# Max-pooling graph layer on one Trainium2 core: own-feature products of 34 node tiles made early, kept in DRAM and added by an identity product

## The chip, the cores and the metric

The program runs on one core of one Trainium2 chip. The metric is device time in microseconds (us) of one execution, from the hardware. Engines are named as in the profile: PE does matrix products (PEld loads their stationary operand), DVE and ACT do elementwise work, POOL issues the indirect gathers, SP and ACT issue direct DMAs (SPq and ACTq are their queues). Sixteen DMA engines move the data. On the printed clock column, PEclk 1.00 is the full TensorE clock.

## The reference

There are N = 6250 nodes with 256 features and E = 100000 edges, sorted by destination. The input is normalised, passed through a ReLU, and sent through four graph layers, then added to x:

```python
h = jnp.maximum(_layernorm(x, axis=-1), 0.0)
def _sage_mean(h, src, dst, n, deg, W_self, W_neigh, b):
    msum = jax.ops.segment_sum(h[src], dst, num_segments=n)
    return h @ W_self + (msum / jnp.clip(deg, 1.0)[:, None]) @ W_neigh + b
def _sage_pool(h, src, dst, n, deg, W_pool, b_pool, W_self, W_neigh, b):
    hp = jax.nn.relu(h @ W_pool + b_pool)
    hmax = jax.ops.segment_max(hp[src], dst, num_segments=n)
    hmax = jnp.where(deg[:, None] > 0, hmax, 0.0)
    return h @ W_self + hmax @ W_neigh + b
...
h = _sage_mean(features, edge_src, edge_dst, n, deg, W1_self, W1_neigh, b1)
h = _sage_pool(h, edge_src, edge_dst, n, deg, W2_pool, b2_pool, W2_self, W2_neigh, b2)
h = _sage_gcn(h, edge_src, edge_dst, n, deg, W3_neigh, b3)
h = _sage_mean(h, edge_src, edge_dst, n, deg, W4_self, W4_neigh, b4)
return h @ W_fc + b_fc
```

The case is about the second layer, `_sage_pool`: for each node the largest of its neighbours' rows `hp[src]`, times one matrix, plus the node's own features times another.

## The kernel before

Nodes lie in 49 tiles of 128 (tile d holds nodes 128d to 128d+127), edges in 782 groups of 128. Layer 1 leaves two tables in DRAM: `tab_p`, the rows `hp` of 512 floats, and `tab_t`, one 128x512 float block a tile that holds, transposed, the tile's normalised features and its neighbour mean (two 128-column pieces of each).

**The edge pass of layer 2** is the loop `for b in reversed(range(NB))` (L1679 on), over six blocks of edges, the last block first. Its counter `at` counts the 782 groups. For each, POOL gathers 128 rows of `tab_p` (256 KB) into a buffer `X` (L1688), DVE takes running maxima along the sorted edges (`step`, L1669: about one and a half instructions a group), and SP stores one of two rows back to DRAM (`rows<-X`, L1673). Six `X` buffers of two groups each rotate; a buffer is free again when its store has landed.

**Work issued beside the pass, at program points given by `at`:**
- up to `MADE_AT` = 64: products of weight matrices (`products2`), which give `usA`, `usB` (own features) and `unf` (maxima);
- `at` 17 to `EARLY_AT` = 310: `build_narrow` makes 14 blocks of an edge-count matrix for layer 3. For each, ACT makes one-hot rows (`ht` L375, `hs` L382), DVE others (`hm` L377), PE multiplies (`pb`, L393), ACT copies out (`A`, L398) and checks (`many`, L408). ACT stores the block (`tab_a`);
- from `at` = 112: `done2(d)` for tiles 48 down to 0, as their edge blocks are finished. `totals(d)` has POOL gather the maxima (`tot`, L1521) and ACT load the tile's `tab_t` block into `th` (L1527, a tag `th2` with four buffers). Then PE turns the maxima (L1545), ACT copies (L1548), PE adds up one PSUM bank `pm_prf`: the own-feature product from `th` with `usA` (L1552) and `usB` (L1555), and the maxima with `unf` (L1558). After that PE and ACT split the result into parts (L1567 to L1598) and ACT stores it (`tab_r`, L1599);
- after `at` = 320: `early_products`, layer-3 products of tiles 0 to 39 in batches of four. SP loads pieces of `tab_a` (`ae`, L1637), ACT widens them (`aw`, L1624), PE multiplies (`pd`, L574), DVE adds up (`acc`, L1306). Their buffers lie where `build_narrow` had its own, so they wait for its end.

The last tiles to be served go through `last_done2`, which places the own-feature product between the steps of the last carry (L1465). A scheduler turns program order into one in-order stream for each engine; within it an engine waits at the head of its stream.

A float product of 128x128 by 128x512 is one call in the code and shows in the trace as two MATMUL instructions; the own-feature product of a tile is four calls, eight instructions.

## Time and profile before

| what | value |
|---|---|
| median of 3 runs | 2745.0 us (2740.99 to 2750.39) |
| the profiled execution's own time | 2742.18 us |
| its span, first to last instruction | 2740.4 us |
| edge pass of layer 2 | first gather at 731.4 us, last at 1923.2 us |
| busy share of the span | PE 84%, DVE 76%, POOL 68%, ACT 47% |
| granted TensorE clock | 0.922 mean |

The profile is of one execution. Busy times of a window are read against its length; the idle time of an engine matters only where another waits for it. A row of the windows view gives, for each engine, busy time and number of instructions in that stretch, then the granted clock, the mean busy share of the 16 DMA engines and the rate that they moved. A row of the groups view gives line, engine, operation, out<-in, number | busy us, mean ns | idle time just before, with what ended it.

### The profile page before, as it was taken

To read this page: it belongs to the slowest core of one execution; us is meant where nothing else is said; L and a number is where in the kernel's file an instruction comes from. 1 tells how busy PE (TensorE), PEld (TensorE's weight loads), DVE (VectorE), ACT (ScalarE), POOL (GpSimd) and SP (SyncE) were. 2 spreads that over 40 slices of the span, in tenths; PEclk is the share of its full clock that TensorE was granted. 3 is DMA by queue.
4 is the path that set the end of the run, shared out by engine and by line. 5 is a ranking of instruction groups with operands and counts; after the bars stand their busy time and mean duration, and the time that the engine had idled before them with its cause. 6 is when DMAs were issued, how large, how long until landed. Compare 5 with 4: busy or idle time off the path is not lost.

```text
span 2740.4 us, 37738 instructions
## 1 busy us (share of the span) xinstructions
PE 2314.7 (84%) x10402; PEld 1439.0 (53%) x10402; DVE 2088.1 (76%) x5540; ACT 1299.7 (47%) x2859; POOL 1857.0 (68%) x2169
## 2 busy tenths in 40 slices
PE   4689999999786466566889999899799999789988
PEld 2356666767453232223555666655345444467776
DVE  8889777776589898898678998888376777446666
ACT  5568777764288888686423333232111111134443
POOL 5477777777566676677656676676477777657765
PEclk8799999999898588787999999999899999899999
DMA  8467777777799899899999999898899999999987
GB/s 279 152 179 209 209 208 213 217 232 221 222 356 333 299 346 336 283 336 361 328 290 301 339 349 322 275 341 292 300 376 387 381 380 351 347 323 316 319 286 226
DMA packets 365625, 809.90 MB, mean 296 GB/s; under 512 B 56238, under 2 KB 154646, under 8 KB 365372
## 3 DMA queue, kind: packets, MB, share of 16 engines
q0 software_dynamic: 143248, 501.86, 56.3%
q1 hardware_dynamic: 145928, 215.57, 21.6%
q10 hardware_dynamic: 76228, 89.96, 9.8%
q8 instruction: 85, 1.39, 0.2%
q14 instruction: 136, 1.11, 0.1%
HBM read 602.51 MB, written 205.46 MB: 295 GB/s over the span
## 4 chain that ended last, share of the span: by engine, by line
PE 48%; DMA 24%; DVE 13%; ACT 5%; issue 4%; POOL 2%; ACTq 0%; DVEq 0%; SPq 0%; POOLq 0%
PE pd L574 17%; PE pg L513 11%; DMA X<-rows,srcIf 7%; DMA xr<-in_x 4%; DVE run L1669 4%; DMA ring<-tab_h,srcT 4%; PE pm_hp L1175 3%; DMA rows<-X 3%; PE pm_prf L1558 3%; PE pm_hp L1169 2%; PE pd L566 2%; PE pb L349 2%; DVE acc L544 2%; DVE X L1669 2%; PE pm_prf L1552 2%
## 5 line engine op out<-in xcount | busy, mean ns | idle before, releaser
L1688 POOL DMA_INDIRECT X<-rows,srcIf x782 | 742.1, 949 | 368.9 <-issue 150.6
L1669 DVE SCALAR_TENSOR_TENSOR run<-run,samef,X 128x512 f32<-128x512 f32 x758 | 572.4, 755 | 49.0 <-DMA X<-rows,srcIf 43.5
L492 POOL DMA_INDIRECT ring<-tab_h,srcT x474 | 455.4, 961 | 149.9 <-issue 53.1
L513 PE MATMUL pg<-ring,hot 128*128 128x259 bf16 (+1 forms) x2292 | 475.1, 316 | 41.9 <-DMA ring<-tab_h,srcT 29.1
L544 DVE SCALAR_TENSOR_TENSOR acc<-pg,M,acc 128x256 f32<-128x256 f32 (+2 forms) x617 | 314.3, 536 | 80.9 <-PE pg L513 69.1
L492 POOL DMA_INDIRECT ring<-tab_r,srcE x290 | 293.3, 1011 | 116.2 <-issue 48.5
L1794 ACT CAST af<-ac 128x768 fp32r<-128x768 fp8e4 (+3 forms) x216 | 173.2, 805 | 398.9 <-DMA ac<-tab_a 157.8
L492 POOL DMA_INDIRECT ring<-tab_s,srcE x266 | 254.6, 957 | 124.6 <-PE pg L510 47.8
L566 PE MATMUL pd<-zt,af 128*128 128x512 f32 x1078 | 302.9, 407 | 38.1 <-ACT af L1794 31.6
L513 PEld LDWEIGHTS <-hot 128*128 128x128 bf16 x2292 | 214.3, 98 | 226.4 <-issue 103.6
L1669 DVE SCALAR_TENSOR_TENSOR X<-X,samef,run 128x512 f32<-128x512 f32 x379 | 282.1, 744 | 37.4 <-DMA X<-rows,srcIf 16.5
L574 PE MATMUL pd<-kept_rows,aw 128*128 128x512 f32 x920 | 292.2, 440 | 11.2 <-ACT aw L1624 6.3
L566 PEld LDWEIGHTS pd<-zt,af 128*128 128x128 f32 x1078 | 208.7, 196 | 95.8 <-ACT af L1794 44.6
L574 PEld LDWEIGHTS pd<-kept_rows,aw 128*128 128x128 f32 x920 | 174.7, 192 | 83.9 <-issue 35.3
L488 DVE TENSOR_SCALAR hot<-iota_bf,keyE 128x128 bf16<-128x128 bf16 (+1 forms) x556 | 142.9, 281 | 86.7 <-PE pg L513 55.3
L1558 PE MATMUL pm_prf<-unf,hTf 128*128 128x512 f32 x384 | 201.0, 647 | 1.9 <-ACT hTf L1548 1.3
L341 ACT ACTIVATE hs<-ht,onef 128x128 bf16<-128x128 bf16 x396 | 153.3, 393 | 89.4 <-PE pb L349 88.4
L1624 ACT CAST aw<-ae 128x512 fp32r<-128x512 fp8e4 x160 | 99.4, 622 | 181.3 <-PE pd L574 163.9
L574 PE MATMUL pd<-Z,A 128*128 128x256 bf16 (+1 forms) x1176 | 184.8, 274 | 0.7 <-ACT A L354 0.6
L375 ACT ACTIVATE ht<-iota_bf,skR 128x128 bf16<-128x128 bf16 x448 | 158.1, 402 | 11.0 <-DMA col<-in_L_gnn_b 8.0
L393 PE MATMUL pb<-hm,hs 128*128 128x196 bf16 x448 | 82.3, 281 | 89.8 <-ACT A L398 65.4
L340 ACT ACTIVATE ht<-iota_bf,sk 128x128 bf16<-128x128 bf16 x396 | 153.1, 398 | 8.3
(391 smaller groups left out, 4198.6 us busy)
## 6 DMA issues: line engine op xcount, KB each, us to landing
rows<-X SPq DMA_DIRECT2D x385, 256.0 KB, 4.9
tab_r<-r ACTq DMA_DIRECT2D x48, 384.0 KB, 5.9
rows<-hpf SPq DMA_DIRECT2D x49, 256.0 KB, 3.4
th<-tab_t ACTq DMA_DIRECT2D x49, 256.0 KB, 6.6
X<-rows,srcIf POOLq DMA_INDIRECT x782
tab_a<-A ACTq DMA_DIRECT2D x14, 784.0 KB, 6.0
ae<-tab_a SPq DMA_DIRECT2D x160, 64.0 KB, 5.0
tab_s<-q SPq DMA_DIRECT2D x39, 256.0 KB, 6.1
```

The lines of the kernel that those rows point to most:

```text
L340: nc.scalar.activation(t, iota_b, AF.Abs, bias=sk[:, r : r + 1])
L341: nc.scalar.activation(hots[0], t, AF.Relu, bias=one, scale=-1.0)
L375: nc.scalar.activation(held["ht"][:, i, :], iota_b, AF.Abs, bias=sk[:, r : r + 1])
L492: nc.gpsimd.indirect_dma_start(out=ring[:, j % deep, :].bitcast(F32) if wide else ring[:, j % deep, :], out_offset=None, in_=table, in_off ...
L513: mm = nc.tensor.matmul(pg[:, : F + c], hot[j], X[:, part * F : (part + 1) * F + c], start=(k == 0 and part == 2), stop=(k == n - 1 and pa ...
L544: nc.vector.scalar_tensor_tensor(acc[d], half, m, acc[d], op0=ALU.mult, op1=ALU.add)
L566: nc.tensor.matmul(hold[0], a, z, start=(s == ss[0]), stop=(s == ss[-1]))
L574: nc.tensor.matmul(hold[0][:, : F + c], a, z[:, part * F : (part + 1) * F + c], start=(first and s != own), stop=(s == ss[-1] and part == ...
L1558: nc.tensor.matmul(pm, hT[:, c, :], un[:, c, :], start=False, stop=(c == KH - 1))
L1669: nc.vector.scalar_tensor_tensor(put, held, st, row, op0=ALU.mult, op1=ALU.max)
L1688: nc.gpsimd.indirect_dma_start(out=X[:, k, :], out_offset=None, in_=tab_p, in_offset=bass.IndirectOffsetOnAxis(ap=srcI[:, t : t + 1], axis=0),
L1794: nc.scalar.copy(wide[i][:, :n, :], got[i][:, :n, :])
```

## The change

For the 34 tiles 33 to 0, the ones that `done2` serves last, the own-feature product is made ahead. A new generator `own_parts` is stepped between `at` = 64 and `at` = 430, eight steps a tile: load the `tab_t` block into a `th2` buffer (`own_rows`), four steps later multiply by `usA` and `usB` into a PSUM bank of the shared three, copy with ACT into another `th2` buffer, and store it on ACT's queue to a new DRAM table `tab_o`. When such a tile is served, `totals` loads its `tab_o` block instead of the `tab_t` block, and `done2` starts the sum with one product of the identity with that block in place of the four calls; one `yield` between them goes too. `last_done2` does the same. Tiles 34 to 48 are served as before.

```diff
+OWN = 34
+OWN_AT = (MADE_AT, 430)
...
+    tab_o = dram.tile([OWN, P, FH], F32, name="tab_o")
...
         def last_done2(d):
...
-            th = wk.tile([P, 2 * KI, P], F32, name="th2", bufs=4)
-            nc.scalar.dma_start(th, tab_t[d].rearrange("p (k n) -> p k n", n=P))
+            op = own_part(d)
...
             def own(to):
-                for k in range(made[0], to):
-                    us = usA[:, k, :] if k < KI else usB[:, k - KI, :]
-                    tc.keep_in_program_order(
-                        nc.tensor.matmul(pm, th[:, k, :], us, start=(k == 0), stop=False))
-                made[0] = max(made[0], to)
+                if not made:
+                    made.append(tc.keep_in_program_order(
+                        nc.tensor.matmul(pm, ident, op, start=True, stop=False)))
...
+        def own_rows(d):
+            th = wk.tile([P, 2 * KI, P], F32, name="th2", bufs=4)
+            nc.scalar.dma_start(th, tab_t[d].rearrange("p (k n) -> p k n", n=P))
+            return th
+
+        def own_part(d):
+            op = wk.tile([P, 2 * KI, P], F32, name="th2", bufs=4).rearrange("p k n -> p (k n)")
+            nc.scalar.dma_start(op, tab_o[d])
+            return op
+
+        def own_parts():
+            for d in reversed(range(OWN)):
+                th = own_rows(d)
+                for _ in range(4):
+                    yield
+                pm = bank(psm, "pm", "pm_own2")
+                for k in range(KI):
+                    nc.tensor.matmul(pm, th[:, k, :], usA[:, k, :], start=(k == 0), stop=False)
+                yield
+                for k in range(KI):
+                    nc.tensor.matmul(pm, th[:, KI + k, :], usB[:, k, :], start=False,
+                                     stop=(k == KI - 1))
+                yield
+                yield
+                op = wk.tile([P, 2 * KI, P], F32, name="th2", bufs=4).rearrange("p k n -> p (k n)")
+                nc.scalar.copy(op, pm)
+                nc.scalar.dma_start(tab_o[d], op)
+                yield
...
-            th = wk.tile([P, 2 * KI, P], F32, name="th2", bufs=4)
-            nc.scalar.dma_start(th, tab_t[d].rearrange("p (k n) -> p k n", n=P))
-            return tots, th
+            return tots, own_part(d) if d < OWN else own_rows(d)
...
-            for k in range(KI):
-                nc.tensor.matmul(pm, th[:, k, :], usA[:, k, :], start=(k == 0), stop=False)
-            yield
-            for k in range(KI):
-                nc.tensor.matmul(pm, th[:, KI + k, :], usB[:, k, :], start=False, stop=False)
+            if d < OWN:
+                nc.tensor.matmul(pm, ident, th, start=True, stop=False)
+            else:
...
             yield
...
+                    if at > OWN_AT[0]:
+                        while own_steps < 8 * OWN * (at - OWN_AT[0]) / (OWN_AT[1] - OWN_AT[0]):
+                            next(owns, None)
+                            own_steps += 1
```

**ACT, while the narrow matrices are built.** The stream of the changed kernel around one early tile (`pm_own` is the bank of the early product; a row without x2 and the like is one instruction):

```order
L1542 COPY th_12383<-pm_own_12323 128x512
L378 ACTIVATE ht<-iota_bf,skR 128x128
L1543 DMA tab_o<-th_12383 128x512
L378 ACTIVATE ht<-iota_bf,skR 128x128
L401 ACTIVATE A<-pb 128x2x49x4
L1519 DMA th_12401<-tab_t 128x512
L378 ACTIVATE ht<-iota_bf,skR 128x128 x2
L401 ACTIVATE A<-pb 128x2x49x4
```

The copy, the store and the next tile's load (L1542, L1543, L1519) are new here; before, only the `ht`, `hs`, `A` and `many` rows and the loads and copies of `done2` stand in this place.

**PE at the same place,** changed kernel: an early tile, and one that is served by `done2` behind it (`hm`, `hs`: the one-hot rows of the narrow build).

```order
L396 MATMUL pb<-hm,hs 128x196
L1537 MATMUL pm_own_12950<-usB,th_12859 128x512 x2
L1572 MATMUL pt_hTf<-identf,tot 128x128 x4
L396 LDWEIGHTS hs
L396 MATMUL pb<-hm,hs 128x196
L396 LDWEIGHTS hs
L396 MATMUL pb<-hm,hs 128x196
L1582 MATMUL pm_prf<-usA,th_12908 128x512 x2
L1585 MATMUL pm_prf<-usB,th_12908 128x512 x2
```

The `pm_own` rows are new between the `pb` rows. PE comes to the first of them when ACT has issued the load of its `th` about three `A` copies earlier in ACT's stream; the loads of `done2` stood about three such copies ahead before and stand five or six ahead now.

**PE in the second half,** among the early products of layer 3 (`kept_rows`, `r_8`, `r_9`: their rows). Before:

```order
L574 MATMUL pd<-r_9_16166,aw 128x512 x2
L1552 MATMUL pm_prf<-usA,th_17460 128x512 x2
L1555 MATMUL pm_prf<-usB,th_17460 128x512 x2
L1558 MATMUL pm_prf<-unf,hTf 128x512 x2
L574 MATMUL pd<-kept_rows,aw 128x512 x2
L1558 MATMUL pm_prf<-unf,hTf 128x512 x2
```

and now:

```order
L577 MATMUL pd<-r_9_16415,aw 128x512 x2
L1579 MATMUL pm_prf<-th_17772,identf 128x512
L1588 MATMUL pm_prf<-unf,hTf 128x512 x2
L577 MATMUL pd<-kept_rows,aw 128x512 x2
L1588 MATMUL pm_prf<-unf,hTf 128x512 x2
```

Four product calls became one. Counted in DVE's stream by its 1161 `step` instructions (L1669), the last one-hot row of the narrow build stood behind the 533rd and now stands behind the 587th, and the first `acc` of the early products behind the 647th and now behind the 717th; the last `acc` stood behind the 1147th and now behind the 1156th.

More of the change, by code (lines that the diff above doesn't have):

```diff
@@ L1455, in last_done2 @@
             tots = [total(d, b) for b in range(1, b_of[d][1] + 1)]
-            th = wk.tile([P, 2 * KI, P], F32, name="th2", bufs=4)
-            nc.scalar.dma_start(th, tab_t[d].rearrange("p (k n) -> p k n", n=P))
+            op = own_part(d)
             pm = bank(psb, "pb", "pm_last")
-            made = [0]
+            made = []
             def own(to):
-                for k in range(made[0], to):
-                    us = usA[:, k, :] if k < KI else usB[:, k - KI, :]
-                    tc.keep_in_program_order(
-                        nc.tensor.matmul(pm, th[:, k, :], us, start=(k == 0), stop=False))
-                made[0] = max(made[0], to)
+                if not made:
+                    made.append(tc.keep_in_program_order(
+                        nc.tensor.matmul(pm, ident, op, start=True, stop=False)))
             def turned(t, name):
@@ L1550, in done2 @@
             pm = bank(psb, "pb", "pm_prf") if apart else bank(psm, "pm", "pm_prf")
-            for k in range(KI):
-                nc.tensor.matmul(pm, th[:, k, :], usA[:, k, :], start=(k == 0), stop=False)
-            yield
-            for k in range(KI):
-                nc.tensor.matmul(pm, th[:, KI + k, :], usB[:, k, :], start=False, stop=False)
+            if d < OWN:
+                nc.tensor.matmul(pm, ident, th, start=True, stop=False)
+            else:
+                for k in range(KI):
+                    nc.tensor.matmul(pm, th[:, k, :], usA[:, k, :], start=(k == 0), stop=False)
+                yield
+                for k in range(KI):
+                    nc.tensor.matmul(pm, th[:, KI + k, :], usB[:, k, :], start=False, stop=False)
             yield
@@ L1678, in fast_path @@
         now = []
+        owns = own_parts()
+        own_steps = 0
         at = 0
```

## The prediction

> **What bounds the kernel now.** I first read the windows view over the edge pass of layer 2 (busy us and instructions of each engine, granted clock, DMA share, GB/s), because all that the change touches lies there:
>
> ```profile
> core 0: us, PE busy (x) PEld busy (x) DVE busy (x) ACT busy (x) POOL busy (x), PEclk, DMA share, GB/s
> 731.00:1930.00 1199.00, 943.06 (x3257) 553.16 (x3257) 1027.89 (x2058) 654.65 (x1395) 800.59 (x843) 0.88 0.94 322
> 820.00:1185.00 365.00, 210.88 (x676) 99.83 (x675) 325.80 (x862) 298.31 (x694) 247.40 (x260) 0.74 0.94 319
> 1185.00:1290.00 105.00, 69.97 (x210) 31.25 (x208) 95.62 (x188) 79.59 (x175) 77.24 (x82) 0.83 0.99 354
> 1290.00:1360.00 70.00, 63.76 (x228) 42.31 (x228) 45.94 (x65) 32.20 (x60) 46.91 (x50) 0.94 0.98 341
> 1360.00:1760.00 400.00, 370.92 (x1354) 243.86 (x1355) 344.33 (x517) 131.85 (x227) 257.73 (x273) 0.97 0.94 315
> 1760.00:1930.00 170.00, 153.77 (x511) 91.18 (x509) 138.31 (x207) 48.99 (x88) 111.24 (x118) 0.95 0.91 310
> ```
>
> The reader is to see two regimes. Up to 1290 us DVE (89% of 820:1185) and ACT (82%) are full and PE is not (58%, at a clock of 0.74). From 1290 us PE is the fullest (93% of 1360:1760), ACT a third busy. DMA is at 0.91 to 0.99 throughout. Then I asked who waits for whom from 1290 to 1800 us, and for the chain of waits there:
>
> ```profile
> SPq L1637 <- ACT aw L1624: 123.9, 97, 7.8
> ACT aw L1624 <- PE pd L574: 136.0, 79, 6.5
> POOL X L1688 <- DMA rows<-X: 24.1, 26, 7.6
> by line: PE pd L574 29.4%; DMA X<-rows,srcIf 13.0%; PE pm_prf L1558 8.8%; issue 6.9%; DMA rows<-X 6.5%; DVE run L1669 6.1%; DMA ae<-tab_a 5.3%; PE pm_prf L1552 4.6%; PE pm_prf L1555 4.4%; DVE X L1669 3.3%; POOL X L1688 2.3%; DMA tot<-rows,r
> ```
>
> So PE reaches the gathers by way of SP's queue: a late `pd` keeps `aw`, that keeps the load `ae` at the head of SP's stream, and the store of `X` behind it, for which POOL's next gather waits. The own-feature product is 4.6 + 4.4 = 9.0% of this chain. The DMA rows behind it (13.0% and 6.5%) are next.
>
> The gathers themselves, POOL's L1688, give the pace and tie `at` to time; and two stretches show what the DMA engines can do:
>
> ```profile
> 820.00:1360.00 540.00, 344.64 (x363) 0.79 0.95 329
> 1360.00:1930.00 570.00, 337.37 (x357) 0.96 0.93 313
> 750.00:850.00 100.00, 88.82 (x335) 49.24 (x336) 92.67 (x247) 81.66 (x190) 66.55 (x71) 1.00 0.99 360
> 1500.00:1650.00 150.00, 150.00 (x544) 95.82 (x543) 138.18 (x200) 54.24 (x94) 105.83 (x112) 1.00 0.98 339
> ```
>
> 363 gathers fit the 366 counts from 64 to 430, so the added work falls on 820 to 1360 us. A gather takes 540/363 = 1.49 us there, 570/357 = 1.60 us afterwards.
>
> **The change part by part.** Prices of single pieces:
>
> ```profile
> 1521.32 1.72 PE pm_prf L1555 x4
> L1558 PE MATMUL pm_prf<-unf,hTf 128*128 128x512 f32 x128 | 81.4, 758 | 1.9 <-ACT hTf L1548 1.3
> L1548 ACT COPY hTf<-pt_hTf 128x512 f32<-128x512 f32 x16 | 9.5, 593 | 0.0
> L1527 ACTq DMA_DIRECT2D th<-tab_t x48: 326/326/413, 781.5 to 1852.5; - x48
> th<-tab_t ACTq DMA_DIRECT2D x49, 256.0 KB, 6.6
> ```
>
> *PE, removed.* Four instructions take 1.72 us when they follow closely, so a tile's own product (eight) takes 3.44 us and the identity product (two) 0.86. For 34 tiles 34 x 2.58 = 88 us go from after 1290 us. *PE, added.* The same eight per tile appear between 820 and 1360 us: 34 x 3.44 = 117 us close up, 34 x 8 x 0.758 = 206 us at the mean of L1558 in 820:1290.
>
> *DMA, added.* Loading `tab_o` takes the place of loading `tab_t`: nothing. New are 34 loads and 34 stores of 256 KB: 68 x 0.262 MB = 17.8 MB, all on ACT's queue; SP's and POOL's get none, but all share the engines. 820:1360 moves 329 x 540 = 177.7 MB today, then 195.5. At 360 GB/s, the fullest stretch, that takes 543 us (+3); at today's 329 it takes 594 (+54); other loads can shift it by little, since each gather brings its own 256 KB. I take the middle, 344.5 GB/s, beside the 339 of the densest later stretch: 567 us, **+27**.
>
> [...]
>
> [...]
>
> *ACT, added.* A copy (0.593) and two issues (0.326 each): 1.245 us a tile, 42 us over all, 28 of the 34 tiles before the build ends. ACT's other work in 820:1290 is the narrow build:
>
> ```profile
> L398 ACT ACTIVATE A<-pb x199: 473/491/575, 823.9 to 1271.2; 128x392 fp8e4<-128x392 f32 x199
> ACT A L398 <- PE pb L393: 50.2, 23, 14.9
> 1288.46 5.33 DMA ae<-tab_a
> PE pm_prf L1552 <- DMA th<-tab_t: 32.7, 11, 5.1
> DVE hm L377 <- PE pb L393: 16.5, 9, 10.7
> PEld pt_hTf L1545 <- ACT r L1598: 10.4, 8, 3.5
> ```
>
> The build ends at 1271 us and the first `ae` load follows at 1288. ACT had 50 us of waits for `pb`, so 28 x 1.245 = 35 us come on top of an engine with little room, and the build ends some 35 us later. It isn't what the gathers wait for, and its delay is priced at 0 there: sixteen `hm` buffers let DVE run ahead of it. But the early products start 35 us later and crowd what PE has gained. In the stream the added store and load stand ahead of `ht` and `A` rows; what waits for those is `pb`, then `hm`.
>
> *The loads' landing.* Eleven `th` loads kept PE 32.7 us, 3.0 each, at the lead of three `A` copies that the 34 new loads have; those of `done2` now lead by more. Bounds: 34 x 3.0 - 32.7 = +69 us of PE, or below nothing (-33) if all land in time; I take the former. In 820:1185 PE has 154 us of room; 23 of the 34 tiles fall there, with 79 to 139 us of products and some 47 of landings. So PE fills up but isn't over, and I price both at 0 on the path (the second rival is what they cost without that room). Sharing three PSUM banks and four `th2` buffers more closely has no row of its own; it costs between 0 and the 1.3 us of one wait of `pt_hTf` for a bank (10.4/8) a tile, on PE again, and I take 0 with the rest.
>
> *1290 to 1360 us.* Here PE is at 64 of 70 us and gets 70/540 x 34 = 4.4 early tiles, 15 us, less 2.5 served ones (6.5 us): 72 of 70, and some waits with it. Between 0 and +9: **+5**.
>
> The served tiles are counted by L1552 (busy and number of PE and PEld, four instructions a tile):
>
> ```profile
> 1290.00:1360.00 70.00, 4.78 (x10) 1.90 (x10) 0.94 0.98 341
> 1360.00:1760.00 400.00, 36.79 (x72) 14.52 (x72) 0.97 0.94 315
> 1760.00:1930.00 170.00, 22.75 (x44) 8.35 (x44) 0.95 0.91 310
> ```
>
> *After 1360 us,* 116/4 = 29 tiles or 75 of the 88 us go. If PE alone set the pace that would be -75; if DMA does, 313 x 570 = 178.4 MB at 344.5 GB/s gives -52; in the dense 1500:1650 DMA share is 0.98 already, and the change is worth at most 2% there. By the chain, 9.0% of 510 us is 46 us, three quarters of it 34. Half comes back: the next links are the DMA rows, and the early products are squeezed by the late build. -17, with -3 for 1800:1930: **-20** (bounds 0 and -52).
>
> *The end.* The last tile drops six instructions of L1465, 3.6 us, which lie beside a landing that the chain waits for:
>
> ```profile
> L1465 PE MATMUL pm_last<-usA,th x4: 592/592/595, 1931.0 to 1932.3; 128*128 128x512 f32 x4
> 1933.94 4.22 DMA tot<-rows,rows_of
> ```
>
> Worth 0, or -3 if that cover were gone. Sum: 27 + 5 - 20 + 0 = +12. The profiled execution took 2742.2 us (2740.4 of it span), which gives 2754; the median of the runs lies 2.8 above it, so **2757 us**, slower by 0.4%.
>
> **Rivals.** *PE's relief wins.* The edge pass runs at 360 GB/s where it is let, and 750:850 made 71 gathers in 100 us (1.41 us each) with the weight loads beside them, so the added bytes fit. Then the first part costs +3, 1290:1360 +2, and the later part gains 40: 2745 - 35 = 2710. For it: PE is 93% busy in 1360:1760, DVE, the next, 86%; and SP's 124 us of waits for `aw`. Against: DMA at 0.93 there and late early products. The clock belongs to it: PEclk was 0.74 with PE at 58%, 0.97 at 93%; own products between the `pb` rows would raise it, and PE's 211 us in 820:1185 would shrink to 211 x 0.74/0.90 = 173 at a clock of 0.90, paying for a third of the added products.
>
> [...]
>
> *PE and ACT choke in the first part.* One mechanism: every new product stands in PE's stream on a load just issued. In 820:1185 PE has 211 us; 23 tiles at 8 x 0.758 add 139, and 23 x 3.0 = 69 of landings: 419 of 365. It decides once PE's work and landings pass 365; then ACT waits for `pb`, DVE for freed `hm` buffers, and the gathers behind them in DVE's stream are late by the 54 us too many, less a few where the clock rises: +45, and the other terms about 0 to +5. 2745 + 50 = 2795. For it: DVE waited 16.5 us for `pb` already. Against it is a stretch with two such landings, one of them shown, that still made 36 gathers, one every 1.39 us:
>
> ```profile
> 1014.26 3.78 PE L1552 MATMUL pm_prf<-usA,th 128*128 128x512 f32 x4 [5.14 <-DMA th<-tab_t]
> 1000.00:1050.00 50.00, 34.09 (x36) 0.81 0.99 356
> ```
>
> *It cancels.* First part +20, later part -20, within 0.3%: 2745. That the change doesn't do what it says is not open; the streams show the products moved.
>
> **How the numbers follow.** The main case, slower by about 12, gets 0.36; choking 0.18; cancelling 0.18; relief 0.28. A measurement of this kernel can tell about 0.3% (8 us) from no change. So slower 0.36 + 0.18 = 0.54, within 0.18, faster 0.28. The range reaches into the relief case and past the choking one's centre: 2716 to 2800. The main case alone would be 2753 to 2778.
>
> **What would show it.** The gathers of counts 64 to 430 should take about 570 us instead of 540, at 340 to 350 GB/s; the last `A` copy should come some 60 us later (35 and the slower pass), `ae` behind it; after that PE should fall below 90% with a gather every 1.55 us. If 64 to 430 takes under 550 us, my first term is wrong and the relief is right; over 590, choking is. Wrong altogether: a changed time outside layer 2.

## The result, and the profile after

The changed kernel takes 2803.16 us (median of four runs, 2797.37 to 2810.55), the kernel before 2742.99: a ratio of 1.0228, 95% interval 1.0207 to 1.0248. It is slower by 60 us, where 12 had been forecast, and 3 us above the end of the stated range. Two later runs of it gave 1.0229 (1.0206 to 1.0253) and 1.0232 (1.0206 to 1.0258). The profiled execution took 2797.37 us.

Of the 55 us by which the profiled span grew (2740.4 to 2795.6), 50 lie in the edge pass of layer 2. In the changed kernel the gathers (POOL's L1720, before L1688) run from 730.1 to 1972.2 us, before from 731.4 to 1923.2: 1242 us for 1192. The other 6 lie behind the last gather and have no single place; the two later runs have them too, and e6 to e8 below don't. From the last gather to the first of layer 3 both kernels need 28 to 29 us. Here is the windows view of the changed kernel, with the columns of the one shown of before (busy us and instructions of PE, PEld, DVE, ACT and POOL, granted clock, DMA share, GB/s):

```profile
731.00:1930.00 1199.00, 928.95 (x3145) 533.84 (x3146) 986.82 (x1988) 657.41 (x1396) 774.11 (x816) 0.88 0.95 325
820.00:1185.00 365.00, 235.76 (x716) 108.31 (x715) 315.60 (x810) 269.72 (x615) 239.61 (x252) 0.81 0.95 330
...
1290.00:1360.00 70.00, 46.66 (x134) 20.92 (x132) 57.79 (x102) 41.77 (x86) 50.02 (x54) 0.80 1.01 375
1360.00:1760.00 400.00, 349.28 (x1236) 226.18 (x1236) 308.83 (x455) 142.65 (x252) 248.56 (x262) 0.94 0.95 318
```

The reader is to see that PE is emptier, not fuller, just where the forecast had it overfull: 47 of 70 us in 1290:1360 (64 before), 87% in 1360:1760 (93% before). POOL, which issues the gathers, did 262 instructions in 1360:1760 instead of 273. The DMA engines are as full as they were (0.95 of 1360:1760, 0.94 before; 0.95 and 0.94 of 731:1930). For what the gathers waited for, here are the two views that the prediction used, SP's wait for `aw` (us in total, times, longest) from 1290 to 1800 us:

```profile
SPq L1667 <- ACT aw L1654: 70.5, 60, 2.4
```

and the chain of waits there, by line:

```profile
by line: DMA X<-rows,srcIf 26.9%; PE pd L577 16.5%; DMA rows<-X 10.9%; issue 10.7%; POOL X L1720 7.0%; DVE run L1699 6.8%; PE pm_prf L1588 5.4%; DVE X L1699 4.1%; DMA ae<-tab_a 2.1%; DVE acc L1309 1.8%; DMA tot<-rows,rows_of 1.5%; PE pm_prf
```

Before, they gave 123.9 us, and a chain that `pd` on PE led with 29.4%, the gathers' own landing (`X`) at 13.0%. It looks as if the path by way of PE, `aw` and SP's queue had been cut in half. But a window of fixed time holds different work: the early products start at 1363 us in the changed kernel and at 1288 before. From gather 430 to the last gather the same views (SP's wait, DVE's waits for the landing of gathers, the chain) give, before:

```profile
SPq L1637 <- ACT aw L1624: 123.6, 95, 7.8
DVE run L1669 <- DMA X<-rows,srcIf: 19.0, 14, 2.8
DVE X L1669 <- DMA X<-rows,srcIf: 6.5, 11, 2.0
by line: PE pd L574 29.8%; DMA X<-rows,srcIf 16.2%; PE pm_prf L1558 8.9%; issue 7.4%; DVE run L1669 6.8%; PE pm_prf L1552 4.7%; PE pm_prf L1555 4.6%; DVE X L1669 3.2%; DMA rows<-X 3.0%; POOL X L1688 2.9%; DMA ae<-tab_a 2.4%; DVE acc L1306 2
```

and after:

```profile
SPq L1667 <- ACT aw L1654: 111.8, 85, 11.1
DVE run L1699 <- DMA X<-rows,srcIf: 52.4, 25, 6.9
DVE X L1699 <- DMA X<-rows,srcIf: 19.7, 20, 3.5
by line: PE pd L577 24.9%; DMA X<-rows,srcIf 20.4%; issue 9.1%; PE pm_prf L1588 8.1%; DMA rows<-X 7.4%; DVE run L1699 6.0%; DMA tot<-rows,rows_of 4.2%; POOL X L1720 3.9%; DVE X L1699 3.5%; DVE acc L1309 2.0%; DMA ae<-tab_a 1.8%; PE pm_prf L
```

`pd` leads in both, and SP's wait fell by 12 us, not by 53. What grew is DVE's wait for gathers to land, from 25.5 to 72.1 us (75 and 82 in e5 and e18; 41, 37 and 36 in e6, e7 and e8). These 47 us are about what this part of the pass lost (42, see below). They say where the time went, not why the gathers landed late.

The narrow build ends later. Its copies `A` and the loads `ae` of the early products behind it (number, shortest, median and longest ns, first and last start):

```profile
L401 ACT ACTIVATE A<-pb x224: 473/488/557, 748.3 to 1337.5; 128x392 fp8e4<-128x392 f32 x112
...
L1667 SPq DMA_DIRECT2D ae<-tab_a x160: 319/320/1542, 1363.0 to 1913.4; - x160
```

The last `A` moved from 1271.2 to 1337.5 us, the first `ae` from 1288.5 to 1363.0. That made the late build the first theory.

**The pass split by gathers.** Counting gathers instead of microseconds puts the same part of the program beside itself. The added work is stepped from count 64 to 430. These rows run from gather 64 to gather 430 and from there to the last, 782, in the kernel before:

```profile
820.30:1364.70 544.40, 344.32 (x1113) 173.29 (x1111) 469.68 (x1118) 409.80 (x927) 374.92 (x394) 0.79 0.95 328
1364.70:1923.30 558.60, 519.61 (x1848) 332.82 (x1849) 473.54 (x711) 178.70 (x310) 364.63 (x386) 0.96 0.93 313
```

and in the changed kernel:

```profile
817.70:1371.30 553.60, 359.87 (x1068) 164.77 (x1067) 472.24 (x1116) 396.19 (x896) 371.93 (x392) 0.80 0.96 336
1371.30:1972.20 600.90, 535.69 (x1942) 351.55 (x1942) 470.42 (x707) 210.36 (x370) 368.00 (x389) 0.95 0.93 309
```

The first part costs 9 us, the later part 42. Time by rate gives the bytes: 178.6 and 174.8 MB before, 186.0 and 185.7 MB after. So the first part moved only 7.4 MB more, although 24 of the 34 added loads and 23 of the stores (12.3 MB) fell in it: other work slipped out, 20 `ae` loads among it. PE ran fewer instructions there (1068 for 1113) in spite of the products added. The rest came later: 10.9 MB more, and 94 more instructions on PE, in a part that the change was to empty. The DMA issues of that later part, before:

```profile
ae<-tab_a SPq DMA_DIRECT2D x127, 64.0 KB, 5.0
th<-tab_t ACTq DMA_DIRECT2D x26, 256.0 KB, 6.6
```

and after:

```profile
ae<-tab_a SPq DMA_DIRECT2D x148, 64.0 KB
th<-tab_o ACTq DMA_DIRECT2D x32, 256.0 KB
tab_o<-th ACTq DMA_DIRECT2D x11, 256.0 KB
th<-tab_t ACTq DMA_DIRECT2D x10, 256.0 KB
```

Eleven of the 34 early tiles are stored only here. There are 27 more transfers of 256 KB (7.1 MB; 21 of the early tiles, 6 for served tiles), and 21 more `ae` loads (1.4 MB), the tail of the late build.

### The profile page after: what moved, and what is told of

Read it like the earlier page. It is cut to its first block, busy times and chain, and to the rows that moved or that the text cites. A ratio compares the mean times of both kernels' runs of the same rounds, so it can differ in the third digit from the quotient of the medians.

```text
span 2795.6 us, 38033 instructions
## 1 busy us (share of the span) xinstructions
PE 2345.4 (84%) x10470; PEld 1451.9 (52%) x10470; DVE 2090.0 (75%) x5540; ACT 1321.4 (47%) x2893; POOL 1858.9 (66%) x2169
## 4 chain that ended last, share of the span: by engine, by line
PE 47%; DMA 27%; DVE 10%; issue 6%; ACT 3%; POOL 3%; ACTq 0%; DVEq 0%; POOLq 0%; SPq 0%
PE pd L577 16%; PE pg L516 11%; DMA X<-rows,srcIf 9%; PE pd L569 4%; DMA ring<-tab_h,srcT 4%; PE pm_hp L1178 3%; DMA rows<-X 3%; DVE run L1699 3%; PE pm_w L280 2%; DMA xr<-in_x 2%; PE pm_hp L1172 2%; PE pm_prf L1588 2%; POOL X L1720 2%; PE pb L352 2%; DVE X L1699 2%
## 5 line engine op out<-in xcount | busy, mean ns | idle before, releaser
L1720 POOL DMA_INDIRECT X<-rows,srcIf x782 | 742.9, 950 | 416.6 <-issue 149.3
L1588 PE MATMUL pm_prf<-unf,hTf 128*128 128x512 f32 x384 | 194.2, 631 | 0.1
L491 DVE TENSOR_SCALAR hot<-iota_bf,keyT 128x128 bf16<-128x128 bf16 x474 | 125.9, 275 | 40.9 <-PE pg L516 39.8
```

Of the source, the lines that this page charges most:

```text
L491: nc.vector.tensor_scalar(hot[j], iota_b, keyT[:, j - jb : j - jb + 1], None, op0=ALU.is_equal)
L1588: nc.tensor.matmul(pm, hT[:, c, :], un[:, c, :], start=False, stop=(c == KH - 1))
L1720: nc.gpsimd.indirect_dma_start(out=X[:, k, :], out_offset=None, in_=tab_p, in_offset=bass.IndirectOffsetOnAxis(ap=srcI[:, t : t + 1], axis=0),
```

## The experiments

Three causes were to be told apart. **A**: ACT's stream, lengthened and held by its own added transfers, ends the build late, and the early products with it crowd the end. **B**: the 17.8 MB themselves. **C**: the own products on PE in the first part. **D** says that the relief of PE is worth nothing. **A'**, in later expectations, is A by way of waits for `th2` buffers.

The runs fell on five chips, and each ratio is to the kernel before on the same chip. On one of them (e5 to e8, e18) that takes 2738 to 2743 us, as in the runs of the result. On the others (e1 to e4, e9 to e17) it takes 3119 to 3164 us; hardly anything there moves the time, and what they say is kept apart below. Expectations written after e4 name the two kinds.

### The chip where the change costs 2.3%

**e5 and e18, the changed kernel again.**

> The changed kernel once more, beside its variants. The first four experiments ran on a chip where the kernel before takes 3122 us instead of 2743, and whose gathers are slower throughout; this run gives the changed kernel's ratio on the chip that the next three have. Theory A (ACT's held stream ends the build late): 1.02 to 1.03 where the gathers go at 1.5 us each, and 1.00 to 1.02 on the slower chip, since the kernel before waits for transfers there in any case. Rival B (bytes): more on the slower chip than on the faster one, above 1.025.

> The changed kernel itself. On the slower kind of chip (the kernel before at 3120 to 3160 us), if its loss is that of transfer engines without room: 0.997 to 1.004, as its kin e1 and e12, and then taking the old products away is worth 1.8 to 2.2% beside the additions (against e2) and nothing without them (e3). If the late build costs wherever it comes: 1.01 to 1.025. On the faster kind: 1.0229 as in e5.

Measured: 1.0229 and 1.0232. The loss is stable there; e18 was meant for the other kind of chip and doesn't tell what the change does on it.

**e6, own transfers on SP's queue.**

```diff
-                th = own_rows(d)
+                th = wk.tile([P, 2 * KI, P], F32, name="th2", bufs=4)
+                nc.sync.dma_start(th, tab_t[d].rearrange("p (k n) -> p k n", n=P))
...
-                nc.scalar.dma_start(tab_o[d], op)
+                nc.sync.dma_start(tab_o[d], op)
```

> As in e1: the two transfers of an own block on SP's queue instead of ACT's. Beside the changed kernel on the same chip. Theory A: 1.5 to 2.5% faster than the changed kernel where that is 1.02 or more, with the last A copy some 40 to 60 us earlier. Rivals B and C: the same time as the changed kernel.

Measured: 1.0213 (1.019 to 1.0236), no gain. The same kernel's last `A` copies and `ae` loads, PE's waits for own loads over the pass, and the windows for gathers 64 to 430, 430 to 782 and the whole pass:

```profile
L401 ACT ACTIVATE A<-pb x224: 473/497/544, 748.3 to 1324.8; 128x392 fp8e4<-128x392 f32 x112
L1668 SPq DMA_DIRECT2D ae<-tab_a x160: 319/320/1766, 1336.4 to 1873.5; - x160
PE pm_own L1535 <- DMA th<-tab_t: 90.3, 20, 12.6
```

```profile
819.40:1397.60 578.20, 395.37 (x1229) 189.04 (x1228) 474.51 (x1118) 413.50 (x932) 374.06 (x394) 0.84 0.94 331
1397.60:1975.60 578.00, 496.00 (x1798) 327.27 (x1817) 473.46 (x713) 194.72 (x340) 365.68 (x387) 0.93 0.93 314
730.40:1975.40 1245.00, 964.96 (x3310) 559.79 (x3329) 1026.46 (x2049) 673.73 (x1429) 799.41 (x842) 0.89 0.94 323
```

The early products begin 27 us sooner than in the changed kernel and end 40 us sooner; PE has 40 us less to do in the later part. And the pass is as long as before this edit, 1245 us for 1242: the later part took 578.0 us for 600.9, the first 578.2 for 553.6. So work that crowds the end isn't needed for a pass of this length.

It is not the test of A that was meant. The last `A` copy came 13 us earlier than in the changed kernel, where A had expected 40 to 60, and it is still 54 us later than before. SP's queue also brought a cost of its own: PE waited 90 us for own loads, with waits of up to 12.6 us, for 54 us (up to 6.0) in the changed kernel. What stayed the same is bytes over time: 191.4 and 181.5 MB, together 372.9 MB in 1156 us, against 371.7 MB in 1154.5 us in the changed kernel. That the time is the same was expected by B and C. That a late build costs is not ruled out.

**e7, the transfers without the products.** Own rows are loaded and stored as they came, and the identity product adds them, so the own-feature product of 34 tiles is left out.

```diff
                 th = own_rows(d)
                 for _ in range(4):
                     yield
...
+                nc.scalar.dma_start(tab_o[d], th.rearrange("p k n -> p (k n)"))
```

> The change without its own products and copies: own rows are loaded and stored to tab_o as they came, on ACT's queue, and at the end they are added by the identity product, so the kernel adds the wrong block to the sums of 34 tiles. All 68 transfers and their waits for th2 buffers stay; 117 us or more of PE work and 20 us of ACT copies go. Theory A: half or more of the loss stays, since ACT's stream still waits with the transfers: ratio 1.005 to 1.02, last A copy 20 to 50 us late. Rival B: as slow as the changed kernel. Rival C (the own products on PE): the loss is gone, 0.985 to 1.00.

Measured: 1.0116 (1.0089 to 1.0143), +31 us. Half of the loss is there with no own product made ahead, and with the relief of PE in place. A had expected 1.005 to 1.02, with the last `A` copy 20 to 50 us late; it came at 1312.8 us, 42 late. B had expected the whole loss, C none: neither came.

**e8, the products without the transfers.** They are made of weights that are in SBUF, copied to a spare tile, and not used; the tiles add the block of `tab_t`, so their own-feature product is left out.

```diff
-                th = own_rows(d)
...
-                    nc.tensor.matmul(pm, th[:, k, :], usA[:, k, :], start=(k == 0), stop=False)
+                    nc.tensor.matmul(pm, usB[:, k, :P], usA[:, k, :], start=(k == 0), stop=False)
...
-                nc.scalar.dma_start(tab_o[d], op)
```

> The converse: the own products are made of blocks of weights that are in SBUF already, and copied by ACT to a spare tile; no transfer is added. At the end the tiles add the block of tab_t by the identity product, which is the wrong block. PE has the change's work in the first half, ACT its copies, the DMA engines nothing new. Theory A: the last A copy within 25 us of the kernel before's, time 0.985 to 1.00 of it. Rival C: 1.015 to 1.025 as in the changed kernel. Rival B: 0.98 to 0.99, the gain of the relief alone.

Measured: 1.0023 (1.0006 to 1.0039), +6 us, with the last `A` copy at 1282.4 us, 11 late. A had expected 0.985 to 1.00, B 0.98 to 0.99, C 1.015 to 1.025: A is nearest, and no gain came. Gathers 64 to 430 and 430 to 782 in e7:

```profile
817.80:1375.80 558.00, 317.68 (x976) 153.79 (x975) 473.07 (x1121) 396.31 (x899) 373.68 (x393) 0.74 0.97 342
1375.80:1941.40 565.60, 485.78 (x1784) 324.61 (x1801) 473.10 (x710) 194.45 (x342) 367.26 (x388) 0.93 0.95 321
```

and in e8:

```profile
819.50:1360.20 540.70, 394.92 (x1247) 191.92 (x1248) 470.73 (x1119) 417.21 (x942) 374.52 (x393) 0.85 0.95 329
1360.20:1924.70 564.50, 489.33 (x1785) 323.01 (x1802) 472.81 (x713) 191.75 (x335) 365.98 (x387) 0.94 0.94 313
```

e8 answers C: with the change's products in PE's stream and 395 us of PE work instead of 344, the first part took 540.7 us, less than before. The products stand there without loads to wait for. e8 also speaks for D: in its later part PE had 30 us less to do than before, the rate was 313 GB/s as before, and the part took 564.5 us instead of 558.6, for 1.9 MB more. Relief of PE by 30 us bought nothing that can be seen.

All five kernels of this chip side by side, gathers 64 to 782 (MB from the rows above, rate the quotient, and the start of the last `A` copy):

| kernel | us | MB | GB/s | PE busy us | last `A` at us |
|---|---|---|---|---|---|
| before | 1103.0 | 353.4 | 320 | 864 | 1271.2 |
| e8, products only | 1105.2 | 354.6 | 321 | 884 | 1282.4 |
| after | 1154.5 | 371.7 | 322 | 896 | 1337.5 |
| e6, on SP's queue | 1156.2 | 372.9 | 322 | 891 | 1324.8 |
| e7, transfers only | 1123.6 | 372.4 | 331 | 803 | 1312.8 |

Four kernels, with the same transfers or 5% more, moved them at one rate within 1%, with the DMA engines 0.93 to 0.96 busy. At 321 GB/s the added 17.8 MB take 55 us; the pass grew by 50. These four fit B. e7 doesn't: with PE emptier by 92 us than in the changed kernel the same bytes went through at 331 GB/s, 31 us sooner (its profiled execution was the fastest of its four, 9 us below their median). So the rate isn't fixed, and bytes at the mean rate are not the whole account.

The last column is a rival that these five don't separate from the bytes: the later the build ends, the longer they take, but for e6 and the changed kernel, which lie 2 us apart. A kernel that delays the build without adding bytes would tell; those that do (e4, e11, e15) ran on other chips.

### The other chips

Here the rows are kept short, because the main finding is that the time stands still. The windows of the whole pass for e1, which is the same kernel as e6:

```profile
852.40:2221.80 1369.40, 1007.97 (x3331) 573.40 (x3329) 1028.50 (x2049) 674.10 (x1429) 798.56 (x842) 0.86 0.88 294
```

The same instructions and 402 MB take 1369 us instead of 1245, with the DMA engines 0.88 busy instead of 0.94. They are less full there; in e13 and e14 below 16.7 MB more passed at no cost (3155.6 and 3160.1 us). What sets the pace there is open.

**e1, own transfers on SP's queue** (the edit of e6).

> The changed kernel with one difference: the load of own rows and the store of the finished block go out on SP's queue instead of ACT's, so a wait for a th2 buffer holds SP's stream and no longer ACT's. Bytes, products and copies are the same. Theory A (ACT's stream, held by the waits of its own added transfers, ends the narrow build some 70 us late, and the early products of layer 3 with it): the last A copy comes back to 1285 to 1310 us (it was 1337.5 in the changed kernel, 1271.2 before), the first ae load to before 1330, and the time to 2730 to 2765 us. Rival B (17.8 MB more for the DMA engines) and rival C (the own products on PE in the first part): both stay as they are, so 2795 to 2810 us. A third outcome, above 2810, would say that SP's queue is no better place: row stores kept behind the same waits.

1.0019 (0.9983 to 1.0054). For the changed kernel on a chip of this kind B had expected more than 1.025 (e5's expectation); this kernel has the same bytes, and that didn't come.

**e2, additions without the gain.** Own blocks are made and stored as in the change; the tiles load `tab_t` and make their products as before.

```diff
-            return tots, own_part(d) if d < OWN else own_rows(d)
+            return tots, own_rows(d)
...
-            if d < OWN:
+            if d < 0:
                 nc.tensor.matmul(pm, ident, th, start=True, stop=False)
```

> The changed kernel without its gain: the own blocks are made and stored as in the change, but nothing reads them, and the served tiles load tab_t and make their products as before. Theory A: the build ends as late as in the changed kernel (last A copy at 1330 to 1345 us) and PE has 88 us more work after 1290, so 2815 to 2850 us. If taking products off PE is worth nothing at the end (rival D), it stays at 2795 to 2810. Rivals B and C give the same late end as the change plus whatever the relief is worth, and don't differ from A here; what differs is where the gathers fall back: by A after 1500 us, by B and C before 1360.

1.0218 (1.0186 to 1.025), the one clear change on these chips. From the last gather on:

```profile
2212.80:2320.00 107.20, 105.70 (x373) 63.57 (x372) 24.50 (x55) 34.39 (x62) 4.71 (x5) 1.00 0.24 80
```

PE is busy for nearly all of these 107 us while the DMA engines are 0.24 busy: here the products that came late are left over behind the last gather.

**e3, e9, e13, e17, the gain alone.** Nothing is made in the first part; the tiles add the block of `tab_t` by the identity product, and the own-feature product is left out.

```diff
-            nc.scalar.dma_start(op, tab_o[d])
+            nc.scalar.dma_start(op, tab_t[d])
...
-        owns = own_parts()
+        owns = iter(())
```

> The change's gain alone: nothing is made in the first half; the 34 tiles load the block of tab_t of the same size and add it by one identity product, so this kernel adds the wrong 256 KB block to those tiles' sums. Theory A: the build ends as before (last A copy at 1265 to 1280 us) and PE is relieved of 88 us behind it: 2690 to 2730 us, a gain of 15 to 50. Rival D (the relief is worth nothing, since DMA sets the pace there): 2735 to 2750.

> As e3, on whichever chip this falls: the gain alone, with the block of tab_t added in place of its product. Taken as a plain sum of parts, e5, e7 and e8 give: transfers less gain = +31 us, products less gain = +7, all together +62, so a gain of 24 us and a time of 2712 to 2720, ratio 0.990 to 0.994. Rival D (the pace after 1390 us isn't PE's, so the relief is worth nothing): 0.997 to 1.003, and then the three parts don't add up but make each other dearer by 20 us or more.

> The gain alone once more (the block of tab_t added in place of its product; nothing made in the first half). On the faster kind of chip: if the parts add up (transfers less gain 31 us, products less gain 7, all 62), the gain is 24 us and the ratio 0.989 to 0.994. Rival D (the relief is worth nothing): 0.997 to 1.003. On the slower kind: 0.997 to 1.001, as in e3 and e9.

> The gain alone (nothing made in the first half, the block of tab_t added by one identity product in place of its product). On the faster kind of chip: if the parts add up, the gain is (31 + 7) - 62 = -24 us, ratio 0.989 to 0.994. Rival D (the relief of PE is worth nothing): 0.997 to 1.003. On the slower kind: 0.997 to 1.001, as in e3, e9 and e13.

0.9993 (0.9966 to 1.0019), 0.9984 (0.9956 to 1.0012), 0.9977 (0.995 to 1.0004), 0.9996 (0.9969 to 1.0023). None of the four fell on the chip where the change loses.

**e4, e11, e15, ballast on ACT** in the kernel before: 136 copies of weights to a spare tile that nobody reads, stepped as `own_parts` is.

```diff
+                for i in range(8):
+                    if i % 2 and i // 2 < 4:
+                        nc.scalar.copy(spare, usA[:, 0, :])
+                    yield
```

> The kernel before with ballast on ACT alone: at the places where the change makes its blocks, four copies of a 128x512 block of weights into a spare tile that nobody reads (136 copies of about 0.6 us, some 81 us), no transfer, no product. Theory A: ACT's stream alone sets the end of the build, so the last A copy comes 45 to 80 us later than 1271 us and the time is 2780 to 2830 us (PE is not relieved here). Rivals B and C: no bytes and no products are added, so 2735 to 2755 us.

> As e4, 136 copies of 0.6 us on ACT in the kernel before, nothing else, on whichever chip this falls. In this kernel's instruction streams the last hm build of the narrow matrices stands behind 584 of the 1161 max steps on DVE, as far back as in the changed kernel (587; 533 before). Theory A (the late build costs by itself): 1.015 to 1.03 where gathers take 1.5 us. Rival B, or a cost that needs both bytes and the late build: 0.997 to 1.006.

> As e11: 136 copies on ACT in the kernel before, no bytes, no products, no gain; the build ends as late as in the changed kernel. On the faster kind of chip, theory A (the late build costs by itself): 1.012 to 1.03. Rival B: 0.998 to 1.005. On the slower kind: 1.002 to 1.004.

1.0026 (0.9997 to 1.0055), 1.0032 (1.0005 to 1.0059), 1.0029 (0.9995 to 1.0063). The last `A` copy comes 29, 65 and 38 us later than in the gain-alone kernel of the same chip (e4 against e3, e11 against e9, e15 against e13). The time is some 9 us over the kernel before, and part of it can be PE work behind the last gather (e15, from the last gather to the last product of the layer); there is no profile of the kernel before on these chips to set beside it:

```profile
2236.50:2306.00 69.50, 67.94 (x247) 41.42 (x247) 23.01 (x48) 20.76 (x37) 4.82 (x5) 1.00 0.29 99
```

**e10 and e14, transfers without buffers behind them.** Loads (7/8 of the size) to one spare tile that nobody reads, stores from a block of weights, no products or copies; the block of weights is added in place of the own-feature product.

```diff
-                th = own_rows(d)
+                nc.scalar.dma_start(spare, tab_t[d][:, : 7 * KI * P // 4])
...
-                nc.scalar.dma_start(tab_o[d], op)
+                nc.scalar.dma_start(tab_o[d], usA.rearrange("p k n -> p (k n)")[:, :FH])
```

> The 68 transfers on ACT's queue with no th2 buffer behind them: each load of own rows (7/8 of the 256 KB) goes to one spare tile that nobody reads, each store to tab_o is taken from a block of weights. No product, no copy; at the end the identity product adds that block, which is the wrong one. Beside e7, where the same transfers pass through th2 buffers. Rival B (the bytes themselves cost): as e7, ratio 1.008 to 1.016. Theory A' (ACT's stream waits for th2 buffers): 0.990 to 1.002, with the last A copy before 1295 us.

> As e10: 68 transfers without th2 buffers behind them, no product, no copy, the gain in place (the wrong block is added). 34 x (0.229 + 0.262) = 16.7 MB. On the faster kind of chip, rival B (bytes): 1.006 to 1.016, as e7's 1.0116. Theory A' (waits for th2 buffers): the gain alone, as e13. On the slower kind: 0.995 to 1.001.

0.9977 (0.9951 to 1.0004) and 0.9981 (0.9945 to 1.0016). On these chips neither the bytes (these two) nor the waits for buffers (e1, with them: 1.0019) showed a cost, so e7's question, which of the two cost there, stays open.

**e16, the same with 32 of the 128 partitions** in each transfer.

> As e14 with 32 of the 128 partitions in each of the 68 transfers: the same number of issues and landings, a quarter of the bytes (4.2 MB), and the block of tab_t added at the end as in e13. On the faster kind of chip, if bytes cost (rival B): a quarter of the way from e13 to e14. If it is the number of transfers, their issues on ACT and what they wait for: as e14. On the slower kind: 0.995 to 1.001.

0.9958 (0.9927 to 0.999), which overlaps with e13 and e14 on that chip. The whole pass in e13 (no added transfer; the profiled execution lies 23 us above the median of its ten):

```profile
864.60:2283.10 1418.50, 916.85 (x3040) 538.56 (x3057) 1025.52 (x2049) 655.73 (x1395) 800.19 (x842) 0.79 0.83 271
```

and in e14 (16.7 MB more):

```profile
865.90:2267.20 1401.30, 919.58 (x3040) 538.17 (x3057) 1026.78 (x2050) 657.35 (x1395) 801.71 (x843) 0.80 0.86 286
```

With the added bytes the rate rose there from 271 to 286 GB/s and the busy share of the DMA engines from 0.83 to 0.86, at no cost that the medians show (3155.6 and 3160.1 us). On the first chip, with the engines at 0.93 to 0.97, every kernel with the added bytes was slower than the kernel before.

**e12, the block copied over its own rows**, so that a tile holds one `th2` buffer and not two; the result is the same.

```diff
-                op = wk.tile([P, 2 * KI, P], F32, name="th2", bufs=4).rearrange("p k n -> p (k n)")
+                op = th.rearrange("p k n -> p (k n)")
```

> The changed kernel with one difference: the finished own block is copied over its own rows in the same th2 buffer, so a tile holds one of the four buffers and not two, and the result is the same. If waits for th2 buffers are what costs (theory A'): 1.000 to 1.012, last A copy before 1310 us. If not (rivals B and C, or the order of the streams, in which the last hm stands behind 588 steps here too): 1.018 to 1.025.

0.9981 (0.9941 to 1.0021). Beside e2 it says that with the additions made, dropping the old products is worth some 2% on this kind of chip (1.0218 in e2, against 1.0019 in e1 on the same chip and 0.9981 here on another), since less is left behind the last gather (from there to the last instruction 968 us in e2, 883 in e1, 897 in e12); without the additions (e3) it is worth nothing.

On the chip where the change loses, no kernel was faster than the kernel before.

## Why the prediction was wrong

The sum was 27 + 5 in the first part, -20 after it, 0 at the end. Measured were +9 (8 and 4 us between the same gathers of e5 and e18), +42 and +6. So the sign was right by luck: the loss was to come in the first part and a gain behind it, and it was the other way round.

*"After 1360 us ... -20."* This is the step that failed, by 62 us. It counted on PE being relieved of 75 us of own-feature products there, and then took most of that back for the DMA rows and the late early products. The relief itself didn't come. PE's groups from gather 430 to the last, before:

```profile
L574 PE MATMUL pd<-kept_rows,aw 128*128 128x512 f32 x760 | 243.3, 440 | 4.1 <-DVE acc L1306 4.1
L574 PE MATMUL pd<-r,aw 128*128 128x512 f32 x360 | 125.5, 454 | 30.1 <-DVE acc L1306 20.2 <-ACT acc L1309 9.9
L1552 PE MATMUL pm_prf<-usA,th 128*128 128x512 f32 x116 | 59.5, 632 | 0.0
L1555 PE MATMUL pm_prf<-usB,th 128*128 128x512 f32 x115 | 54.1, 592 | 0.0
```

and after:

```profile
L577 PE MATMUL pd<-kept_rows,aw 128*128 128x512 f32 x910 | 287.6, 442 | 15.9 <-DVE acc L1309 10.8 <-ACT acc L1312 5.0
L577 PE MATMUL pd<-r,aw 128*128 128x512 f32 x348 | 119.2, 447 | 33.5 <-DVE acc L1309 30.0 <-ACT acc L1312 3.3
L1579 PE MATMUL pm_prf<-th,identf 128*128 128x512 f32 x62 | 31.9, 596 | 0.0
L1534 PE MATMUL pm_own<-usA,th 128*128 128x512 f32 x40 | 21.9, 677 | 0.0
L1537 PE MATMUL pm_own<-usB,th 128*128 128x512 f32 x40 | 19.7, 618 | 0.0
```

Own features took 113.6 us before and take 73.5 now, 40 less and not 75, since 41.6 us of early tiles' products came only here; and 38 us more of early products (`pd`) had slipped in from the first part. In all PE was busy 536 us for 520. "363 gathers fit the 366 counts ..., so the added work falls on 820 to 1360 us" is the assumption behind it: the stepping by counts sets the place in the program, and 11 of the 34 stores and 10 loads came after count 430. The 10.9 MB more that this part moved would make 35 of its 42 us at 313 GB/s; that they are the reason is argued, not shown. What a relief of PE is worth there is not measured alone on this chip; e8, with 30 us less on PE, shows nothing.

*"DMA, added ... I take the middle, 344.5 GB/s ...: 567 us, +27."* As a price of the first part this was too high: gathers 64 to 430 took 553.6 us at 336 GB/s, since the part moved 7.4 MB more and not 17.8. The rate is a middle between two stretches, and over gathers 64 to 782 no such rate was reached (320 GB/s before, 322 after). At 322 the 17.8 MB are 55 us, the prediction's own upper bound, and the pass grew by 50; e7 shows that the agreement doesn't prove the rate.

*"The build ends some 35 us later ... priced at 0"*, 60 us with the slower pass. The build's delay was 66 us, close to what was named. Pricing it at 0 fits the first part (+9), but what it pushed back is part of what the later part had to carry, and no run on this chip prices the delay alone.

*"PE, added ... the loads' landing ... I price both at 0 on the path."* Right for the first part. PE's waits for own loads in 820:1290 of the changed kernel:

```profile
PE pm_own L1534 <- DMA th<-tab_t: 53.9, 17, 6.0
```

That is 3.2 us each, as priced; PE's clock rose from 0.74 to 0.81 in 820:1185, and e8 shows the first part no longer for 51 us more of PE work. The choking rival, whose 2795 came nearest to the time, was wrong in its mechanism: the gathers were 9 us late at count 430, not 45. e6 comes nearer to it: with longer waits of PE for own loads, its gathers were 34 us late there.

*"1290 to 1360 us, +5"*, from PE at 72 of 70 us. Wrong: PE had 46.66 us, because the work due there had slipped. *The end, 0*: 6 us, in the two repeats too. Of the signs that the prediction named, PE did fall below 90% (87%), but with a gather every 1.71 us (600.9 us for 352) and not every 1.55.

What the runs show of the cause is this. Products alone don't cost the time (e8: +6 us). The transfers without the products cost half of it (e7: +31). Sending the transfers by another queue doesn't save it (e6: 1.0213). So the loss came only with the transfers, but how they cost is open: as bytes (in a pass whose DMA engines were 0.94 busy before and are 0.95 busy now, the 17.8 MB are 4.6% more bytes and go with 4.2% more time), or as waits in the streams that end the build late, by 42 us in e7 and 66 in the changed kernel. Open is also the other half: either the relief of PE has a worth of some 25 us that e8 doesn't show, or products that wait for loads and loads that wait for buffers make each other dearer by as much. The gain alone, the ballast and the transfers without buffers would tell on this chip, and all of them ran on others.

## What to carry to other kernels

Where the DMA engines are as busy over a whole stage as here (0.93 to 0.97 of both parts of the pass, in all five kernels), price added bytes at the stage's mean rate, not at that of its densest stretch, and call it an estimate (55 us at 321 GB/s; the change lost 60, the transfers alone 31). At 0.83 to 0.86 busy, on another chip, 16.7 MB showed no cost (e13 and e14). Look for the bill in the whole stage: here the stretch that took most of the transfers lost 9 us, and the later one, into which other work had slipped, 42. Before counting on an engine that is relieved, ask what will slip into the room: here PE got more to do (536 us for 520) where it was to get less. Compare kernels by the count of the pacing instruction (here the gathers), with bytes and busy time for each piece: the same window of time holds other work once something has moved, and its chain of waits then misleads (SP's wait for `aw` fell by 53 us in the window and by 12 between the same gathers).

## What the runs showed that was not expected

**Chips differ.** The same kernel took 2738 to 2743 us on one chip and 3119 to 3164 on the others. The row of rates in 40 slices of the page of the changed kernel (e18, first kind of chip):

```profile
GB/s 273 155 182 207 206 209 221 225 221 221 259 350 307 334 365 342 302 326 373 337 292 298 314 340 338 299 290 300 258 371 387 376 385 360 336 316 320 318 283 234
```

and of e1 (another chip, own transfers on SP's queue):

```profile
GB/s 272 136 159 174 174 175 186 179 173 179 182 283 281 273 303 303 300 312 300 316 303 321 284 296 307 282 268 279 222 352 355 356 352 347 327 322 281 273 274 201
```

In slices 3 to 10, among the gathers of layer 1, the rates are 159 to 186 GB/s instead of 182 to 225, and the best slice is 356 instead of 387. No run tells why.

**Rates above 360 GB/s.** The prediction's fullest stretch, 750:850, went at 360. The changed kernel held 375 GB/s for the 70 us of 1290:1360, and the page of e18 above has a slice at 387. The page of the kernel before had shown such rates: four of its 40 slices, among the gathers of layer 3, went at 376, 387, 381 and 380.

**A wait that names another queue.** In 820:1290 ACT stood idle until row stores of SP's queue had landed; the view names the next counted instruction, and in the stream one of ACT's own transfers stands between. In the changed kernel:

```profile
ACT ht L378 <- DMA rows<-X: 22.7, 9, 4.7
ACT many L411 <- DMA rows<-X: 16.1, 7, 5.9
```

and in e8, which adds no transfers:

```profile
ACT ht L378 <- DMA rows<-X: 18.2, 6, 4.6
ACT many L411 <- DMA rows<-X: 11.1, 3, 5.0
```

Before, these two rows came to 3.8 us. They looked like the cause of the late build, yet e8 has three quarters of them, with its last `A` at 1282.4 us and no loss in the first part. So a wait that had grown from 3.8 to 29.3 us was no cost there that the time of the first part shows (540.7 us, 544.4 before).
